# Sixteen-expert transformer layer on one core: four scattered tiles normalised one gate pair earlier, and one output product put off by a step

## The chip, the cores and the metric

The kernel runs on one NeuronCore of a Trainium2 chip, in one launch. The metric is the device time in microseconds (us). A profiled execution gives, beside that time, a span (first to last instruction) and a record of every instruction of every engine: PE (TensorE, with its weight loads as PEld), DVE (VectorE), ACT (ScalarE), POOL (GpSimd) and SP (SyncE, which here only issues DMAs).

## The reference, cut to what matters

Four blocks follow each other on x of 2048 rows (8 batches of 256) by 512 columns, each with a layer norm in front and a residual sum behind. Only the last two are near the change.

```python
x = x + _L0_xattn_ref(ctx_2048, ctx_2048, _layernorm(x, axis=-1), ...)
x = x + _L0_ffn_ref(_layernorm(x, axis=-1), ...)
x = x + _L1_xattn_ref(_layernorm(x, axis=-1), ctx_2048, ...)   # 16 heads, then out @ Wo + bo
x = x + _L1_ffn_ref(_layernorm(x, axis=-1), ...)
```
```python
def _L1_ffn_ref(x, wa, rg, rgb, rw1, rb1, rw2, rb2, sg, sgb, sw1, sb1, sw2, sb2):
    # each expert: (gelu(x @ g + gb) * (x @ w1 + b1)) @ w2 + b2, 512 -> 256 -> 512
    aff = jax.nn.sigmoid(jnp.einsum('bsd,de->bse', x, wa))
    topk_p, topk_i = jax.lax.top_k(aff, K)          # K = 2 of E = 16
    topk_p = topk_p / jnp.sum(topk_p, axis=-1, keepdims=True)
    combine = jnp.sum(jax.nn.one_hot(topk_i, E, dtype=x.dtype) * topk_p[..., None], axis=2)
    routed = jnp.einsum('bsed,bse->bsd', _experts_all(x, rg, rgb, rw1, rb1, rw2, rb2), combine)
    shared = jnp.sum(_experts_all(x, sg, sgb, sw1, sb1, sw2, sb2), axis=2)   # SH = 2 shared experts
    return x + shared + routed
```

## The kernel before, in words

The 2048 rows are 16 tiles of 128 (tile t is half t % 2 of batch t // 2) and stay in on-chip memory as `xs`. Every engine works its instructions off in a fixed order: inside an `in_order` block the order in the code is the order on PE, DVE, ACT and POOL. So an instruction that waits holds up all that is behind it on its engine.

**Attention (steps).** `steps` has 64 entries: batch b, half i, column pair cp, part p. The loop over n (lines 1363 to 1440 or so) runs a software pipeline: in pass n, POOL normalises the probabilities of step n-1 (`normalise`, L1275, fed by DVE's reciprocal `rden`, L1273), scores of new steps are made (`scores`, L1250), the probabilities of step n-2 are transposed on PE (`turn`, tile `pt`, L1286, copied out by DVE L1293 and ACT L1291), every second pass the value product (`values`, tile `o`, L1305, copied by ACT into `oT`, L1309) of step n-3 runs, and when step n-4 was the last of a half, `project_out` multiplies `oT` by Wo (tile `fo`, L1317, four times 128x512) and DVE adds `fo` to `xs` (L1320). A dictionary `put_off` names halves whose `project_out` waits for a later pass, counted from the start of the last batch; before the change it holds one, `(B - 2, 0): 1`. In the last eight passes and behind them (`at` = n - 56), the first eight tiles are also normalised for the next block by ACT (L1414), transposed on PE (tile `dxT`, L162) and copied by DVE (L1353). The tiles `o`, `fo` and `dxT` share two PSUM buffers ("mm"). After the loop, PSUM is handed to the next pool, whose first products (`lgT`, L1527) wait for DVE's last add.

**Shared experts and routing.** For the first eight tiles (tb 0 and 1) the two shared experts run: for each (tb, e, f) a pair of products `gate` (tile `gu`, L1546: four 128x512 matmuls each, which the trace shows as eight records), ACT's Gelu (L1558) and DVE's `gated` (L1559, tile `yT`). Between the pairs the generator `route` (pieces) is advanced with `next(pieces)`: six pieces work out the two experts of every row and the place `slot` of each row in a buffer `xd` in DRAM; then 16 pieces, one for each tile t, in each of which DVE normalises the tile (L1512, tile `dxs`, a ring of 8 buffers), POOL issues two indirect DMAs that scatter its rows to `xd` (L1675), and DVE brings the tile of `xs` itself to its normalised residual form (L1683). A last piece, called the tail here (L1689 to L1698: `over`, `past`, `expf`, `expert`), works out which expert each overflow block belongs to.

Then `down` (tile `po`, L1568) makes the eight down products, one for each tile of tb 0 and 1, eight records each, and DVE adds each to `xs` (L1572). `po` has four PSUM buffers: the fifth product must wait for the add of the first. After each of the first two down products up to two pieces are taken, as long as there are any.

**Routed experts.** SP loads the scattered rows (`r_xr`, L1710), reads `expert` into registers and loads weights; PE then runs 21 units (`turn`, `products`, `back`). At the end the second half of the shared experts runs while POOL gathers the routed rows.

What the change and the prediction touch: L1357 (`put_off`), L1847 (the counts of pieces), L1273, L1275, L1286, L1305, L1309, L1317, L1320, L1353 in the attention, and L1512, L1559, L1568, L1572, L1675, L1683, L1689 to L1698, L1884 (POOL's sum of the shared biases to every tile) behind it.

## Time and profile before

| | |
|---|---|
| time, median of 3 runs | 1144.72 us (1142.27 to 1147.37) |
| the profiled execution's own time | 1144.64 us |
| its span | 1142.8 us |
| PE busy | 1097.9 us, 96% of the span |
| DVE busy | 685.5 us, 60% |
| ACT busy | 519.4 us, 45% |
| POOL busy | 445.8 us, 39% |
| PE clock granted | 9 tenths or more in all 40 slices |
| HBM traffic | 107.66 MB read, 44.43 MB written |

The profiled execution's time is 1.8 us above its span, and within 0.1 us of the median of the runs. "Busy" is the time in which an engine has an instruction under way; "idle before" in a row is how long the engine had nothing before it, with what ended that idle time behind the arrow. In a timeline, rows of the same kind that follow each other are merged: "13.90 ... x32" is one stretch of 32 records. Source lines are those of the kernel before; in the changed kernel every line from 1355 on is one lower, since an empty line was taken out.

### The profile page before, as it was taken

What the parts mean: (1) busy time and instruction counts of PE and PEld (TensorE: products, weight loads), DVE (VectorE), ACT (ScalarE), POOL (GpSimd) and SP (SyncE); (2) the same over time, 40 slices, a digit from 0 to 9 for tenths busy, and PEclk for the clock granted to TensorE, in tenths of its full rate; (3) what the DMA queues carried; (4) which work ended last, traced back from release to release, by engine and by line L of the source; (5) the groups of instructions that cost most, each with busy time, mean ns of one, the idle gap of its engine ahead of it and who ended that gap; (6) DMA issues with size and microseconds to landing.
All of it is one profiled execution on the core that took longest, in us unless ns stands there. A gap on an engine that the chain in (4) does not pass through costs nothing.

```text
span 1142.8 us, 16506 instructions
## 1 busy us (share of the span) xinstructions
PE 1097.9 (96%) x5885; PEld 659.4 (58%) x5885; DVE 685.5 (60%) x1507; ACT 519.4 (45%) x1176; POOL 445.8 (39%) x501
## 2 busy tenths in 40 slices
PE   4999998899999999999999999899999999999997
PEld 3777776445545555555555555554466666675443
DVE  5998999899865565765656756647332222212452
ACT  4437645798984655756556557530011121111000
POOL 5787887245531333433333435413770000000650
PEclk9999999999999999999999999999999999999999
DMA  7424520799500100000000010053568999997571
GB/s 271 158 75 143 162 75 20 239 304 291 145 1 19 38 1 17 4 19 1 20 19 1 2 37 1 1 195 119 223 206 294 304 331 337 298 309 238 158 248 40
DMA packets 122780, 153.26 MB, mean 134 GB/s; under 512 B 7481, under 2 KB 81273, under 8 KB 122178
## 3 DMA queue, kind: packets, MB, share of 16 engines
q1 hardware_dynamic: 108608, 116.49, 32.2%
q10 hardware_dynamic: 8962, 18.85, 4.6%
q0 software_dynamic: 5120, 16.78, 4.3%
q8 instruction: 49, 0.80, 0.3%
q14 instruction: 41, 0.34, 0.1%
HBM read 107.66 MB, written 44.43 MB: 133 GB/s over the span
## 4 chain that ended last, share of the span: by engine, by line
PE 73%; DVE 19%; POOL 2%; issue 2%; ACT 2%; DMA 0%; ACTq 0%; POOLq 0%; DVEq 0%
PE r_h L1731 10%; PE gu L1546 10%; PE y L713 5%; PE v_mm L885 5%; PE r_po L1747 5%; PE q_mm L885 5%; PE po L1568 4%; PE f_op L493 4%; PE k_mm L885 3%; PE fo L1317 3%; PE pt L1286 3%; PE f_hp L409 3%; DVE mx L1258 2%; PE sc L1250 2%; PE o_h L1788 2%
## 5 line engine op out<-in xcount | busy, mean ns | idle before, releaser
L1275 POOL TENSOR_TENSOR pr<-pr,rden 128x1024 f32<-128x1024 f32 x64 | 121.1, 1893 | 218.9 <-DVE rden L1273 213.3
L713 PE MATMUL y<-kv,tp 128*128 128x288 f32 x640 | 161.7, 408 | 5.3 <-DVE wl L736 5.1
L713 PEld LDWEIGHTS y<-kv,tp 128*128 128x128 f32 x640 | 119.0, 190 | 42.5 <-PE y L713 10.1
L1266 ACT ACTIVATE pr<-sc,mx 128x256 f32<-128x256 f32 x256 | 118.3, 483 | 8.2 <-DVE mx L1258 6.9
L1889 POOL DMA_INDIRECT yg<-yd,slot x32 | 32.9, 1030 | 222.7 <-PE gu L1546 204.4
L1731 PE MATMUL r_h<-r_xT,r_gu 128*128 128x256 f32 x512 | 113.5, 380 | 0.0
L1731 PEld LDWEIGHTS r_h<-r_xT,r_gu 128*128 128x128 f32 x512 | 96.9, 190 | 20.6 <-issue 8.0
L1258 DVE TENSOR_REDUCE mx<-sc 128x4 f32<-128x1024 f32 x64 | 77.6, 1213 | 4.7 <-PE sc L1250 4.5
L1738 DVE SCALAR_TENSOR_TENSOR r_y<-r_h,eb,r_ge 128x256 f32<-128x256 f32 x32 | 15.5, 484 | 95.5 <-PE r_h L1731 95.5
L1286 PE MATMUL pt<-ident,pr 128*128 128x128 f32 x512 | 69.6, 279 | 2.2 <-POOL pr L1275 1.3
L1291 ACT COPY pts<-pt 128x512 f32<-128x512 f32 x64 | 37.8, 591 | 69.3 <-PE pt L1286 69.3
L1286 PEld LDWEIGHTS pt<-ident,pr 128*128 128x128 f32 x512 | 55.1, 140 | 19.1 <-issue 14.6
L1737 ACT ACTIVATE r_ge<-r_h,gb 128x256 f32<-128x256 f32 x32 | 15.1, 473 | 108.9 <-PE r_h L1731 108.9
L409 PE MATMUL f_hp<-w1q,f_xq 128*128 128x512 bf16 x256 | 60.5, 379 | 2.6 <-ACT f_h L422 1.5
L651 POOL TENSOR_TENSOR kv<-kx 128x2048 f32<-128x2048 f32 x16 | 57.6, 3601 | 13.1 <-ACT kx L637 13.1
L1317 PE MATMUL fo<-Wo_sb,oT 128*128 128x512 f32 x128 | 57.9, 595 | 1.1 <-ACT oT L1309 1.0
L885 PE MATMUL k_mm<-Wk_sb,cx 128*128 128x512 f32 x128 | 58.1, 598 | 0.6
L493 PE MATMUL f_op<-w2q,f_hq 128*128 128x512 bf16 x256 | 57.9, 379 | 0.0
L885 PE MATMUL v_mm<-Wv_sb,cx 128*128 128x512 f32 x128 | 57.7, 593 | 0.0
L1747 PE MATMUL r_po<-r_w,r_y 128*128 128x512 f32 x128 | 57.7, 593 | 0.0
L885 PE MATMUL q_mm<-Wq_sb,xT 128*128 128x512 f32 x128 | 57.6, 593 | 0.0
L1558 ACT ACTIVATE ge<-gu,gb 128x512 f32<-128x512 f32 x16 | 11.0, 687 | 100.6 <-PE gu L1546 71.9
(487 smaller groups left out, 2116.9 us busy)
## 6 DMA issues: line engine op xcount, KB each, us to landing
xd<-blank SPq DMA_DIRECT2D x1, 15360.0 KB
tp<-kpd SPq DMA_DIRECT2D x32, 256.0 KB
r_gu<-in_rg SPq DMA_DIRECT2D x16, 512.0 KB
r_gu<-in_rw SPq DMA_DIRECT2D x16, 512.0 KB
r_w<-in_rw SPq DMA_DIRECT2D x16, 512.0 KB
r_xr<-xd SPq DMA_DIRECT2D x16, 512.0 KB
yd<-r_yo ACTq DMA_DIRECT2D x32, 256.0 KB
yd<-blank SPq DMA_DIRECT2D x1, 6144.0 KB
```

Source lines behind the costliest of these rows:

```text
L409: nc.tensor.matmul(dst, lhsT=self.xq[:, i, c, :], rhs=w1q[:, c, cols], start=(c == 0), stop=False)
L493: nc.tensor.matmul(op, lhsT=self.hq[i][:, c, :], rhs=w2q[:, c, :], start=(c == 0), stop=(c == FC - 1))
L713: nc.tensor.matmul(y[:, ll, :, 0:PAIRS], lhsT=tp[:, dl : dl + P], rhs=view(kv, (m0 * G + hh) * PAIRS, [[G * PAIRS, B], [1, PAIRS]]), start ...
L885: nc.tensor.matmul(t, lhsT=lT[:, c, i * P : (i + 1) * P], rhs=w[:, c, :], start=(c == 0), stop=(c == DC - 1),)
L1258: nc.vector.tensor_reduce(self.mx, self.sc.rearrange("p r c k -> p (r c) k"), AX.X, ALU.max, negate=True)
L1266: nc.scalar.activation(self.pr[:, h // 2, h % 2, :], self.sc[:, h // 2, h % 2, :], AF.Exp, bias=self.mx[:, h : h + 1], accum_out=self.den[ ...
L1275: nc.gpsimd.tensor_tensor(flat, flat, rden.unsqueeze(2).to_broadcast([P, 4, S]), ALU.mult)
L1286: nc.tensor.transpose(pt[:, cc, k, :], self.pr[:, rr, cc, k * P : (k + 1) * P], ident)
L1317: nc.tensor.matmul(fo, lhsT=oT[:, c, :], rhs=wsb["Wo"][:, c, :], start=(c == 0), stop=(c == DC - 1))
L1546: nc.tensor.matmul(ps, lhsT=w[0][:, c, k, f * P : (f + 1) * P], rhs=xTs[tb][:, c, :], start=(c == 0), stop=(c == DC - 1),)
L1731: nc.tensor.matmul(ps, lhsT=self.w[0][:, c, k, f * P : (f + 1) * P], rhs=self.xT[:, c, 0:n], start=(c == 0), stop=(c == DC - 1),)
L1747: nc.tensor.matmul(po, lhsT=self.y[:, f, i * P : (i + 1) * P], rhs=self.w[1][:, f, :], start=(f == 0), stop=(f == EC - 1),)
```

## The change

Two numbers of the program's order are changed. The instructions of every engine are the same in number and kind; only their order on PE, DVE, ACT and POOL differs in two places, and SP's queue is the same.

```diff
-
-        put_off = {(B - 2, 0): 1}
+        put_off = {(B - 2, 0): 1, (B - 1, 0): 8}
...
     rest = [(tb, e, f) for tb in range(2) for e in range(SH) for f in range(EC)][2:]
-    for (tb, e, f), n in zip(rest, (0, 2, 3, 3, 3, 3)):
+    for (tb, e, f), n in zip(rest, (0, 2, 3, 3, 4, 4)):
         first_gate = gate(tb, e, f, shw[e], 0)
         for _ in range(n):
             next(pieces)
```

The first: `project_out` of half 0 of the last batch moves from pass n = 63 to n = 64. On PE this is the `fo` product of four 128x512 matmuls: before, it stood between the transposes `pt` of step 61 and the transposes `dxT` of tile 6; after, it stands behind the transposes of step 62 and the value product `o` of steps 60 and 61, ahead of `dxT` of tile 7 and `pt` of step 63. On DVE its add moves behind the copy of tile 6, the reciprocal of the last step and a copy of `pts`; on POOL nothing changes place.

The second: of the 16 scattering pieces, 3, 3, 3 and 3 stood in the four last gate pairs, two (tiles 12 and 13) behind them, and tiles 14 and 15 behind the first down product; the tail stood behind the second. After, 3, 3, 4 and 4 stand in the gate pairs, tiles 14 and 15 stand behind them ahead of all down products, and the tail stands between the adds of the first and the second down product. On DVE the order around the down products is then:

```
before: yT  t12 t13  po0  t14 t15  po1  tail  po2 po3 po4 ...
after:  (t10 t11 t12 t13) yT  t14 t15  po0  tail  po1 po2 po3 po4 ...
```

Here t12 stands for the pair L1512, L1683 of tile 12, and po0 for the add L1572 of the first down product.

## The prediction, made before the changed kernel was run

> **What bounds the kernel now.** I read the page's span and chain first, then the busy time by stage, then the timelines of PE, DVE and POOL around both edits.

> ```profile
> span 1142.8 us, 16506 instructions
> PE 73%; DVE 19%; POOL 2%; issue 2%; ACT 2%; DMA 0%; ACTq 0%; POOLq 0%; DVEq 0%
> 690.00:742.00 52.00, 47.77 (x472) 30.39 (x464) 35.13 (x68) 33.56 (x111) 24.51 (x14) 1.00 0.00 1
> 742.00:810.00 68.00, 67.41 (x243) 33.16 (x244) 39.34 (x95) 14.90 (x24) 22.18 (x40) 1.00 0.51 178
> 810.00:841.00 31.00, 27.99 (x65) 11.75 (x64) 13.85 (x21) 0.00 (x0) 23.12 (x22) 1.00 0.55 198
> 841.00:1050.00 209.00, 208.54 (x912) 143.89 (x910) 45.59 (x82) 38.99 (x79) 11.09 (x9) 1.00 0.90 297
> ```

> The stretches show length, then busy time of PE, PEld, DVE, ACT, POOL, the granted clock (1.00), DMA share and GB/s. From the end of the attention on, PE sets the time. The first edit lies at 726 to 742 us, the second at 800 to 841. Behind 841 PE waits 0.5 us in all until the end (its list of waits has one row there), so what PE gains or loses ahead of 841 goes through to the end unchanged. Of the 31 us with the down products PE is idle 3.0; that is all the second edit can win there, but for the refilling of PE after a wait.

> The end of the attention, PE, then POOL:

> ```profile
> 726.08 1.04 PE L1286 MATMUL pt<-ident,pr 128*128 128x128 f32 x8
> 728.12 3.70 PE L1317 MATMUL fo<-Wo_sb,oT 128*128 128x512 f32 x8 [1.00 <-ACT oT L1309]
> 731.65 0.60 PE L162 MATMUL dxT<-ident,dxn 128*128 128x128 f32 x4
> 732.09 1.04 PE L1286 MATMUL pt<-ident,pr 128*128 128x128 f32 x8
> 735.35 1.09 PE L1286 MATMUL pt<-ident,pr 128*128 128x128 f32 x8 [0.62 <-POOL pr L1275]
> 736.37 1.81 PE L1305 MATMUL o<-pts,v 128*32 128x128 f32 x32
> 738.11 3.70 PE L1317 MATMUL fo<-Wo_sb,oT 128*128 128x512 f32 x8
> ...
> 728.89 1.89 POOL L1275 TENSOR_TENSOR pr<-pr,rden 128x1024 f32<-128x1024 f32 x1 [4.11 <-DVE rden L1273]
> 733.40 1.90 POOL L1275 TENSOR_TENSOR pr<-pr,rden 128x1024 f32<-128x1024 f32 x1 [2.62 <-DVE rden L1273]
> ```

> The product that is moved (728.12) covers exactly the time in which POOL normalises the step whose transposes come next (728.89 to 730.78). The down products, PE, then DVE:

> ```profile
> 810.13 13.90 PE L1568 MATMUL po<-s_w,yT 128*128 128x512 f32 x32
> 824.87 3.70 PE L1568 MATMUL po<-s_w,yT 128*128 128x512 f32 x8 [0.85 <-DVE xs L1572]
> 829.14 3.70 PE L1568 MATMUL po<-s_w,yT 128*128 128x512 f32 x8 [0.57 <-DVE over L1689]
> 834.43 7.13 PE L1568 MATMUL po<-s_w,yT 128*128 128x512 f32 x16 [1.59 <-DVE xs L1572]
> ...
> 824.13 0.69 DVE L1572 TENSOR_TENSOR xs<-xs,po 128x512 f32<-128x512 f32 x1 [8.29 <-PE po L1568]
> 828.40 0.69 DVE L1572 TENSOR_TENSOR xs<-xs,po 128x512 f32<-128x512 f32 x1 [1.49 <-issue]
> 831.31 2.25 DVE L1697 TENSOR_SCALAR expf<-expf 128x56 f32<-128x56 f32 x1
> ```

> The four first products run through in 13.9 us, one each 3.43 us, so the first is done at about 813.7. DVE is free from 815.83 (end of tile 13's L1683), yet its add starts at 824.13, 0.1 us behind the end of the fourth product; the next waits another 1.49 us although its product was done at about 817.2. The last yT before them is late too: 812.97, for a gate product that ended at about 810.3. So most of PE's idle time here does not come from DVE's order, but from PE's completions reaching DVE late. The trace's record of PE's semaphore updates agrees: after 800 it has 812.88, 824.11, then 831.96, 832.05 and 832.14 together, with no product ending just before the first and the last three. I compared every wait of DVE and ACT for PE with the end of the matmul waited for; no other is over 0.4 us late.

> **First edit, the output product.** No instruction is added; I replay PE with the readiness times above. `pt` of step 61 ends at 727.12. Next is now `dxT` of tile 6: it takes the PSUM buffer that ACT's copy of `oT` releases at 728.07, so it runs 728.12 to 728.56. Next is `pt` of step 62, which needs POOL's product, done at 730.78: POOL started it at 728.89 because `rden` stood on DVE at 728.55 behind the batch's moments, and nothing of that is moved. So PE, which had 3.4 us of the moved product here, is idle 2.27 us (728.56 to 730.83). Then `pt` 1.0 and `o` 1.0 to 732.85, the moved `fo` 3.43 to 736.3 (its buffer: tile 6's copy, on DVE 731.6 to 732.3), `dxT` 0.43, `pt` of step 63 from 736.7 to 737.75. The wait of 0.62 for POOL is gone, as POOL starts that step at 732.5. The last `o` reads the `pts` that DVE copies; DVE now has the add of `fo` (736.55) and the copy of tile 7 (0.6 each) ahead of it, so the copy ends at 738.4 (736.73 before). 28 of the 32 products follow, 1.0 us: the last `fo` starts at 739.5, where it was 738.11. Sum: +1.4 us. POOL's sum of the bias (L1327, 1.26) moves behind the last normalisation and has until 742. Bounds: if both old waits went and no hole came, -1.6 (1.00 + 0.62); if the whole hole counts and the last `o` waits its 0.7 more, +3.0. I take +1.4, which the rows give in order.

> **Second edit, the tiles.** Per tile DVE has 0.54 + 0.55 us, in all 1.05 with the pitch; gate pairs take 6.87, and DVE is idle 2.9 us or more before each of the last yTs, so the fourth tile is covered. Each `dxs` needs a ring buffer whose scatter was issued eight tiles earlier: the latest, tile 15, needs tile 7's (its second scatter was issued by 807.66 and its completions stand at 809.4 at the latest) and comes at about 815. POOL's 32 scatters are 1.27 us apart and set its pace; DVE is ahead of them. POOL's only gap, 2.57 us before tile 14 (822.98 to 825.55), goes, so its scatters end 2.6 us earlier; SP's loads of `r_xr` (issued at 832.77, needed at 841.4) come as much earlier. Neither was on PE's path.

> What is on the path is when buffers of `po` come free. Here one thing is unknown: whether the late completions come again. Let the clock run from the first down product.
> - They come again at the same distances (first at 14.0 us, second at 18.3, third at 21.8): the fifth product starts at 14.74 as before. The tail follows the first add. It took 4.6 us before, of which L1697 took 2.25 for 56 elements a partition, beside two POOL additions (L1884, 831.01 to 833.50). Ahead of the scatters' end these POOL additions aren't there, so L1697 is put at 0.2, near its equal neighbours of 0.15 to 0.19 (L1689, L1698), and the tail at 2.5: 14.6 to 17.1. The second add comes at 18.3, the sixth product at 19.0 as before, the third add at 21.8, and the seventh product no longer waits (1.59 plus 0.1 to refill): -1.7.
> - They don't come: no buffer is ever late, the eight products take 8 x 3.43 = 27.5 instead of 31.3 (810.13 to 841.40): -3.8.
> I take -1.7, since the one execution shown has them; -3.8 and the slow rival's +4.7 are the bounds.

> Forecast: 1144.64 + 1.4 - 1.7 = 1144.3 us, no change.

> [...]

> **Rivals.** (a) The late completions are chance of this execution. Then the second edit gives -3.8 and the sum is 1144.64 + 1.4 - 3.8 = 1142.2. For it: no other wait of DVE or ACT for PE in the trace is late like this. Against: the execution's time equals the median of the others.

> (b) Slower. PE's completions reach DVE only where POOL's stream of scatters pauses: the first came at 824.11, in POOL's gap that tile 14 made, and the third to fifth after POOL's last scatter (830.98). The edit removes this gap: the stream then ends at 830.98 + 1.4 - 2.6 = 829.8, completions come about 1.0 later, at 830.8. PE has then been idle since 811.5 + 13.9 = 825.4; the fifth product starts at 831.5 (6.1 idle). Now the tail runs beside POOL's additions, 4.6 us, so the second add ends at 836.8 against the fifth product's end at 834.9: 1.9 more. With two refills of 0.25 that is 8.5 against 3.8: +4.7, and 1144.64 + 1.4 + 4.7 = 1150.7. It decides from the point where the first add starts later than 1 us behind the fourth product's end. Against: from 786 to 807 the scatters ran too and nothing was late.

> (c) The first edit makes no hole and both its waits go: -1.6, with (a) 1144.64 - 1.6 - 3.8 = 1139.2. Against: `rden` at 728.55 is fixed by DVE's order. That the change does not do what it says can't be: the built programs' orders show both moves.

> **How the numbers follow.** About 0.5% (5.7 us) is what a measurement of this kernel can tell from no change: 1139.0 to 1150.4. Forecast 0.48, (a) 0.26, (b) 0.16, (c) 0.10. Inside the 0.5% lie the forecast, (a), most of (c) and a little of (b). Faster by more: 0.07, the part of (c) and chance below 1139.0. Slower by more: 0.13 from (b). Range: from 1140.5, between (a) and (c), to 1149.5, short of (b).

> **What would show it.** The first edit: PE idle about 2.3 us ahead of the second-last `pt` of the attention, with POOL `pr` behind the arrow, and no wait at the last. The second: the first add of `po` ahead of the tail, L1697 short, no PE wait ahead of the seventh down product, and `r_xr` issued earlier. The forecast is wrong if a PE wait appears behind 841, or if the fifth down product waits longer than 0.85 us.

## The result, and the profile after

The changed kernel takes 1150.45 us (median of 6 runs, 1150.16 to 1151.5), the kernel before 1144.91 in the runs beside it (1142.27 to 1147.37). The ratio is 1.0050, with a 95% interval of 1.0034 to 1.0066: slower by 5.5 us. The forecast was 1144.3 us.

The profiled execution after has a span of 1148.7 us, 5.9 more than before. First the same stages as in the prediction (their bounds set anew, by hand, where the work lies now), then three short windows; columns are length, busy time of PE, PEld, DVE, ACT and POOL, granted clock, DMA share and GB/s.

```profile
span 1148.7 us, 16505 instructions
690.00:742.00 52.00, 46.81 (x467) 30.54 (x460) 34.71 (x67) 33.56 (x111) 24.55 (x14) 0.97 0.00 1
742.00:812.50 70.50, 69.72 (x249) 33.88 (x248) 41.65 (x99) 14.90 (x24) 22.04 (x40) 1.00 0.48 170
812.50:847.20 34.70, 29.88 (x66) 12.57 (x65) 11.03 (x17) 0.00 (x0) 22.91 (x22) 0.95 0.51 181
847.20:1056.00 208.80, 208.34 (x911) 143.78 (x909) 45.58 (x82) 38.99 (x79) 11.10 (x9) 1.00 0.90 297
722.87:726.29 3.42, 3.42 (x24) 2.35 (x20) 2.14 (x3) 0.85 (x3) 1.89 (x1) 0.50 0.00 0
832.10:835.51 3.41, 0.74 (x2) 0.30 (x2) 1.44 (x4) 0.00 (x0) 0.42 (x2) 1.00 0.42 145
835.51:838.93 3.42, 3.42 (x5) 1.35 (x4) 1.42 (x3) 0.00 (x0) 3.42 (x4) 0.50 0.84 263
```

From the first down product to `r_xTp` it is now 34.5 us (31.3 before), and twice PE ran at half its clock (0.50) for 3.4 us. The second time follows a window in which PE was busy for 0.74 of 3.41 us. Nothing of this kind lies in the span of the kernel before until its last microseconds.

The end of the attention, PE:

```profile
724.22 1.97 PE L1286 MATMUL pt<-ident,pr 128*128 128x128 f32 x8
727.68 1.04 PE L1286 MATMUL pt<-ident,pr 128*128 128x128 f32 x8
729.66 0.65 PE L162 MATMUL dxT<-ident,dxn 128*128 128x128 f32 x4 [0.94 <-ACT oT L1309]
731.80 1.33 PE L1286 MATMUL pt<-ident,pr 128*128 128x128 f32 x8 [1.50 <-POOL pr L1275]
734.07 3.70 PE L1317 MATMUL fo<-Wo_sb,oT 128*128 128x512 f32 x8
739.75 1.07 PE L1305 MATMUL o<-pts,v 128*32 128x128 f32 x28 [0.33 <-DVE pts L1293]
```

The hole that the prediction placed is there: PE waits for POOL's `pr` ahead of the second-last `pt`. The moved product stands at 734.07. The `pt` of 1.97 us at 724.22 ran at half clock; it lies ahead of the edit, and two kernels without this edit have such a stretch at the same place (e2 from 722.13, e11 from 721.91).

The down products, PE, then DVE:

```profile
812.77 13.90 PE L1567 MATMUL po<-s_w,yT 128*128 128x512 f32 x32
828.82 3.70 PE L1567 MATMUL po<-s_w,yT 128*128 128x512 f32 x8 [2.15 <-issue]
835.19 12.26 PE L1567 MATMUL po<-s_w,yT 128*128 128x512 f32 x24 [2.67 <-DVE xs L1571]
847.29 1.91 PE L162 MATMUL r_xTp<-ident,r_xr 128*128 128x128 f32 x16
...
817.64 0.75 DVE L1558 SCALAR_TENSOR_TENSOR yT<-gu,eb,ge 128x512 f32<-128x512 f32 x1 [6.39 <-PE po L1567]
828.08 0.69 DVE L1571 TENSOR_TENSOR xs<-xs,po 128x512 f32<-128x512 f32 x1 [7.51 <-PE po L1567]
830.98 1.30 DVE L1696 TENSOR_SCALAR expf<-expf 128x56 f32<-128x56 f32 x1
834.45 2.48 DVE L1571 TENSOR_TENSOR xs<-xs,po 128x512 f32<-128x512 f32 x4 [1.93 <-remote]
```

PE's work is unchanged, and its completions (the semaphore updates that tell DVE that a product is done) are late again, but the distances are longer: the first product is done at about 816.4 (812.77 + 3.6), its add starts at 828.08, 15.3 us behind the start of the first product (14.0 before); the second add comes at 21.7 us (18.3 before), and then four adds run at once. The fifth product waits 2.15 us (0.85 before).

What lies on POOL in that time, before and then after:

```profile
822.02 0.96 POOL L1675 DMA_INDIRECT xd<-dxs,slot  x1 [0.30 <-issue]
825.55 1.14 POOL L1675 DMA_INDIRECT xd<-dxs,slot  x1 [2.57 <-DVE dxs L1512]
...
828.70 0.96 POOL L1674 DMA_INDIRECT xd<-dxs,slot  x1 [0.30 <-issue]
829.97 0.96 POOL L1674 DMA_INDIRECT xd<-dxs,slot  x1 [0.30 <-issue]
830.95 1.28 POOL L1883 TENSOR_TENSOR xs<-xs,srow 128x512 f32<-128x512 f32 x1
```

Before, the first add (824.13) came in the pause that ends at 825.55. After, the scatters follow each other at 0.30 us up to 830.93; the first add came in the middle of them and the second 3.5 us behind their end.

So the 5.9 us of span are, in order: 1.0 for the half-clock window at 722.87 (it puts the `pt` behind the hole at 731.80, where e17 below, at full clock up to there, has it at 730.86), 1.6 for the hole in the attention (the first products behind it, `lgT`, start 2.64 later, less the 1.0), and 3.2 in the down products, of which 1.7 is the half-clock window at 835.51 (3.42 us at half speed). Behind 847 PE waits 0.5 us, as before.

### The profile page after: what moved, and what is told of

Its sections match the earlier page's. It is cut to its first block, busy times and chain, and to the rows that moved or that the text cites. A ratio compares the mean times of both kernels' runs of the same rounds, so it can differ in the third digit from the quotient of the medians.

```text
span 1148.7 us, 16505 instructions
## 1 busy us (share of the span) xinstructions
PE 1101.2 (96%) x5885; PEld 661.5 (58%) x5885; DVE 684.5 (60%) x1507; ACT 519.4 (45%) x1176; POOL 445.6 (39%) x501
## 4 chain that ended last, share of the span: by engine, by line
PE 74%; DVE 19%; POOL 2%; ACT 2%; issue 1%; DMA 1%; SPq 1%; another core or an unknown queue 0%; ACTq 0%; POOLq 0%; DVEq 0%
PE r_h L1730 10%; PE gu L1545 10%; PE y L713 5%; PE v_mm L885 5%; PE r_po L1746 5%; PE q_mm L885 5%; PE po L1567 5%; PE f_op L493 4%; PE k_mm L885 3%; PE fo L1317 3%; PE pt L1286 3%; PE f_hp L409 3%; DVE mx L1258 2%; PE sc L1250 2%; PE o_h L1787 2%; PE o L1305 2%
## 5 line engine op out<-in xcount | busy, mean ns | idle before, releaser
L1275 POOL TENSOR_TENSOR pr<-pr,rden 128x1024 f32<-128x1024 f32 x64 | 121.1, 1893 | 219.3 <-DVE rden L1273 211.6
L1286 PE MATMUL pt<-ident,pr 128*128 128x128 f32 x512 | 70.7, 281 | 3.0 <-POOL pr L1275 2.2
L1286 PEld LDWEIGHTS pt<-ident,pr 128*128 128x128 f32 x512 | 55.8, 142 | 20.5 <-issue 14.9
L1317 PE MATMUL fo<-Wo_sb,oT 128*128 128x512 f32 x128 | 57.9, 595 | 0.1
```

The lines of the kernel that those rows point to most:

```text
L1275: nc.gpsimd.tensor_tensor(flat, flat, rden.unsqueeze(2).to_broadcast([P, 4, S]), ALU.mult)
L1286: nc.tensor.transpose(pt[:, cc, k, :], self.pr[:, rr, cc, k * P : (k + 1) * P], ident)
L1317: nc.tensor.matmul(fo, lhsT=oT[:, c, :], rhs=wsb["Wo"][:, c, :], start=(c == 0), stop=(c == DC - 1))
```

## Experiments

Times are ratios to the kernel before, run beside each kernel on the same chip, with 95% intervals; "first add" is the start of the first `po` add, counted from the start of the first down product (3.6 is on time); "waits" is PE's idle time between the down products; "stage" runs from the first down product to `r_xTp`, both from the profile. A run without a ratio is one execution alone; e4, e7, e8, e9 and e16 leave scatters out or shorten them, so they do not compute the whole layer. e1 to e4 ran on one chip, e5 to e8 on a second, e9 to e12 on a third, e13 to e16 on a fourth, e17 and e18 on a fifth.

| run | ratio | span us | first add | waits | stage |
|---|---|---|---|---|---|
| before | | 1142.8 | 14.0 | 3.0 | 31.3 |
| after | 1.0050 (1.0034 to 1.0066) | 1148.7 | 15.3 | 4.8 | 34.5 |
| e1_putoff | 1.0023 (1.0008 to 1.0038) | 1147.6 | 13.3 | 3.3 | 33.2 |
| e2_counts | 1.0023 (1.0008 to 1.0039) | 1147.7 | 17.5 | 4.4 | 34.3 |
| e3_tail_late | 1.0037 (1.0023 to 1.0052) | 1152.1 | 11.8 | 5.0 | 35.7 |
| e4_scatter_8 | | 1142.2 | 3.6 | 0 | 27.5 |
| e5_eight_po | 0.9968 (0.9955 to 0.998) | 1140.9 | 16.3 | 0 | 28.4 |
| e6_counts_eight | 1.001 (0.9997 to 1.0022) | 1147.0 | 21.2 | 4.1 | 35.0 |
| e7_short_rows | | 1152.0 | 21.2 | 8.0 | 37.4 |
| e8_one_scatter | | 1141.7 | 10.7 | 0 | 27.5 |
| e9_last_eight | | 1142.2 | 3.6 | 0 | 27.5 |
| e10_code_shift | | 1161.2 | 3.6 | 0 | 27.5 |
| e11_counts_22 | 1.0001 (0.9991 to 1.001) | 1140.4 | 3.6 | 0 | 27.5 |
| e12_counts_22_eight | 0.9997 (0.9988 to 1.0007) | 1138.9 | 3.6 | 0 | 27.5 |
| e13_after_again | 1.0092 (1.0071 to 1.0114) | 1152.6 | 22.0 | 8.9 | 38.8 |
| e14_counts_22_again | 0.9973 (0.9958 to 0.9987) | 1139.1 | 7.2 | 0 | 27.5 |
| e15_counts_22_eight_again | 0.9971 (0.9956 to 0.9987) | 1139.2 | 6.5 | 0 | 27.5 |
| e16_last_eight_again | | 1141.5 | 3.6 | 0 | 27.5 |
| e17_putoff_22 | 0.9983 (0.997 to 0.9996) | 1142.5 | 10.3 | 0 | 27.7 |
| e18_counts_22_third | 0.9949 (0.9933 to 0.9965) | 1138.9 | 6.3 | 0 | 27.5 |

### Each edit alone, and the tail's place

```diff
# e1_putoff
-        put_off = {(B - 2, 0): 1}
+        put_off = {(B - 2, 0): 1, (B - 1, 0): 8}
# e2_counts
-    for (tb, e, f), n in zip(rest, (0, 2, 3, 3, 3, 3)):
+    for (tb, e, f), n in zip(rest, (0, 2, 3, 3, 4, 4)):
# e3_tail_late: both, and ahead of the tail
+        for _ in range(2):
+            yield
         nc.vector.tensor_copy(over, end[:, E : E + 1])
```

> Only the first edit: the output product of half 0 of the last batch is put off from step 63 to 64; the counts stay 3, 3. Theory A (each edit costs by itself; of the 5.9 us between the two profiled spans the first gives 1.6, the down products 3.3, and a half-clock stretch near 723 us the last 1.0): 1.0 to 2.0 us over the kernel before in the same job, with PE idle about 2 us ahead of the second-last pt and the sixteen tiles' scatters as before, the first add of po at about 14.0 us from the first down product. Rival B (the first edit shifts the routing against the down products and so causes the longer waits there too): 4 to 6 us over before, with the fifth down product waiting 2 us or more.

> Only the second edit: counts 3, 3 become 4, 4, the output product stays where it was. Theory A: 1.5 to 4 us over before, PE idle 2 us or more ahead of the fifth down product, again 2 us or more ahead of the sixth with DVE's add of po behind the arrow and the tail (over, past, expf, expert) ahead of that add; the attention as before. Rival B (the down products wait only when both edits meet): within 0.7 us of before or faster.

> The changed kernel, with two empty pieces ahead of the tail, so that the tail (over, past, expf, expert) stands behind the add of the second down product, where it stood before the change. If the tail's place is what delays the sixth product: 1.5 to 3 us below the changed kernel (1147.5 to 1149), with the second add right behind the first and no second wait. If the second completion of PE reaches DVE late by itself (as the third to fifth, which came together at 834.5 in the changed kernel's trace, 3.6 us behind the last scatter's end): within 0.7 us of the changed kernel, and the second add still stands at 21 us or more behind the start of the first down product, now with DVE idle before it.

Each edit alone costs 0.23%, 2.6 us, and the sum, 0.46%, agrees with the 0.50% of both within the intervals. For e1 that is more than theory A's 1.0 to 2.0; what the rest is, the pair e17 and e18 shows. (In e1's profile the down products are 1.9 us longer too; in that pair PE waits nowhere between them.) In e2 the first add comes at 17.5 us and the fifth product waits 4.4; the expected second wait is not there, since the fifth product ran at half clock (827.95 to 834.77) and so ended behind the second add (833.78). The late tail (e3) changes nothing that can be told (0.37%, against 0.50% for the changed kernel on another chip): the second add still stands 21.6 us behind the start, now with DVE idle for 9.2 us before it. The tail's place is not the cause.

### Is it POOL's stream of scatters?

```diff
# e4_scatter_8, on the changed kernel
-            for k in range(2):
+            for k in range(2 if t < 8 else 0):
# e8_one_scatter: range(2 if t < 8 else 1); e9_last_eight: range(0 if t < 8 else 2)
# e7_short_rows
-                    out=xd, out_offset=offset(ap=slot[:, k, t : t + 1], axis=0),
-                    in_=xn, in_offset=None,
+                    out=xd if t < 8 else xs32, out_offset=offset(ap=slot[:, k, t : t + 1], axis=0),
+                    in_=xn if t < 8 else xn[:, 0:32], in_offset=None,
```

> The changed kernel without the sixteen scatters of tiles 8 to 15 (their rows are then not in the scattered table; the normalising on DVE and everything else stays). Theory S (PE's completions reach DVE late while POOL's stream of scatters runs): with no scatter after about 800 us the last yT and all adds of po start within 0.4 us of the end of their products, the first add about 3.6 to 4.5 us from the start of the first down product, no wait of PE between the down products, and some 5 to 7 us less than the changed kernel (1143 to 1146). Rival D (late completions belong to PE and DVE at this place, whatever POOL does): the last yT is still 3 us late, the first add still stands at 14 us or more from the first down product.

> The changed kernel, whose scatters of tiles 8 to 15 move 32 of the 512 columns of each row, into a table of their own (so the rows of these tiles are not in the scattered table): as many scatters and descriptors on POOL, a sixteenth of the bytes. If the bytes that move hold PE's completions back: on time as without these scatters, the eight products in 27.6 us. If it is POOL's issue or the number of descriptors: the first add still 13 to 17 us behind the start of the first down product, PE waiting 2 us or more.

> The changed kernel with one scatter instead of two for tiles 8 to 15 (the second rows of these tiles are not in the table). If a stream without pauses is what holds completions back: the stream from 810 us on is half as long (eight scatters, about 10 us, over by 820 to 822), so completions are late up to then and on time from then: the first add 8 to 11 us behind the start of the first down product, before the fourth product has ended, and no wait of PE. If each completion waits for a fixed count of scatters or a fixed time: the first add still at 13 us or more.

Without the later sixteen scatters every completion is on time and PE runs the eight products in one stretch (e4, PE):

```profile
813.38 27.63 PE L1568 MATMUL po<-s_w,yT 128*128 128x512 f32 x64
```

With half of them (e8) the stream ends at 821.8, and the adds come at 823.52 and then together; those of products that end later are on time. The bytes are not the cause: with a sixteenth of them (e7) it is worse, the first add comes 3.2 us behind the last scatter's end (831.25). (`xs32` is a table of 32 columns.) Theory S (POOL's stream holds the completions back) stands, and theory D (it belongs to this place on PE and DVE) falls.

### Eight buffers: take away what makes PE wait

```diff
# e5_eight_po, on the kernel before; e6_counts_eight the same with counts 4, 4
-        po = pd.tile([P, D], F32, tag="po", name=f"po{t}")
+        po = pd.tile([P, D], F32, tag="gh" if tb == 1 else "po", name=f"po{t}")
```

> The kernel before, with the down products of tiles 4 to 7 in the four PSUM buffers of the gate products (tag gh), which nothing uses there, in place of a second turn of the four po buffers; orders of all engines as before. Theory S (the scatters hold back PE's completions, and PE loses time only because it needs a po buffer back): the adds still come 10 us late, but PE runs the eight products through in 27.6 us without a wait, and with no stretch of low PE activity there no half-clock window follows near 830 us: 3 to 6 us below before (1140 to 1142.5). Rival T (PE's wait only moves: r_xTp and the next gates need the gh buffers, whose adds are late): a new wait of 2 us or more ahead of r_xTp or of r_h, and within 1.5 us of before.

> The same eight buffers together with the second edit (counts 4, 4), without the first. Theory S: as with 3, 3 within 1 us, since what the second edit costs is only the longer wait for po buffers: 1140 to 1143. If the second edit costs something beside the buffers: 2 us or more above the run with 3, 3.

With counts 3, 3 the completions are as late as ever (first add 16.3 us), but PE has no buffer to wait for, and the kernel is 0.32% faster; 1.0 us of wait for `r_xr` is left ahead of `r_xTp`. With counts 4, 4 the expectation missed by 5 us: 1147.9 instead of 1140 to 1143. PE has buffers and still stops. Its rows in e6:

```profile
810.79 15.61 PE L1568 MATMUL po<-s_w,yT 128*128 128x512 f32 x36
827.05 0.59 PE L1568 MATMUL po<-s_w,yT 128*128 128x512 f32 x1 [0.65 <-issue]
829.14 0.59 PE L1568 MATMUL po<-s_w,yT 128*128 128x512 f32 x1 [1.50 <-issue]
830.54 0.92 PE L1568 MATMUL po<-s_w,yT 128*128 128x512 f32 x1 [0.81 <-issue]
```

After 36 records PE goes on one record at a time, waiting for nothing that the profile names, until the completions come through at 831.9. What the second edit costs is thus not only a buffer: it takes the pause out of POOL's stream. In e5 POOL paused for 4.90 us from 823.5, and six held completions came through together (PE's semaphore updates at 826.94 to 827.32); in e6 there was no pause, and they came at 831.93 and later, 3.2 us behind the last scatter.

### A pause in the right place: the opposite of the second edit

```diff
# e11_counts_22 (again: e14, e18); with eight buffers: e12, e15
-    for (tb, e, f), n in zip(rest, (0, 2, 3, 3, 3, 3)):
+    for (tb, e, f), n in zip(rest, (0, 2, 3, 3, 2, 2)):
# e10_code_shift, on the changed kernel
+    dm = pd.tile([P, TB], F32, tag="po", name="dm")
+    for _ in range(44):
+        nc.tensor.matmul(dm[:, 0:1], lhsT=ident, rhs=ident[:, 0:1], start=True, stop=True)
     pieces = route()
```

> The changed kernel with the scatters of tiles 8 to 15 alone (those of tiles 0 to 7 are left out, so these rows are not in the table): sixteen scatters, from about 802 to 822 us. If the number of scatters before counts (late only from the seventeenth on): the last yT, all adds of po on time, no PE wait. If the place counts, that is what PE does at this point: the last yT and the first add late as in the changed kernel, up to some 2 to 3.5 us behind the last scatter (first add 10 to 13 us from the start of the first down product).

> The changed kernel with 44 tiny products on PE (128x1, into a buffer nobody reads) ahead of the routing, about 745 us. They move the point at which PE's next block of instructions is fetched (16 KB packet on PE's instruction queue, 814.6 in the changed kernel, 2 us behind the start of the down products) some 19 us forward against PE's work, into the gate products of 792 to 800, where scatters run too. Theory F (completions are held back when a fetch of PE's code meets the scatters): late completions start there, gate products wait for gelu and yT, and DVE's normalising with them: the gates take several us longer than the 27 us they took. Theory C (it belongs to the later scatters or to the down products, whatever is fetched): the gates run as before and the last yT and first add of po are late as before.

> The opposite of the second edit, without the first: counts 2, 2 instead of 3, 3, so that tiles 12 and 13 wait for the first add of po and POOL's scatters pause some 5 us earlier (after tile 11, about 818). If a pause of POOL's stream lets the completions through 0.3 to 3.5 us later: the first add at 8 to 12 us from the start of the first down product instead of 14, the second at once behind it, no wait of PE ahead of the fifth and sixth products; the later adds are held again until the last scatter is through, and the seventh product waits 1 to 4 us. In time 2 us below to 1 us above before. If the pause has nothing to do with it: first add at 13 us or later again, and as everything behind it comes later, 3 us or more above before.

> Counts 2, 2 with the eight buffers for the down products. With the pause inside the stream, PE should run the eight products in 27.6 us without a wait; what remains is whether r_xr (loaded behind the last scatter) is in time for r_xTp. Within 1 us of the run with 3, 3 and eight buffers (1142 to 1144). If the later end of the scatters decides: a wait ahead of r_xTp of 2 us or more and 1145 or more.

In all four of these runs every completion was on time, also with a stream without pauses (e10, e11, e12), so they tell nothing of their questions (the span of e10 holds its tiny products and the half-clock stretch that they brought). They ran on a chip on which the kernel before took 1142.1 us (at most 1143.1), where it took 1145.5, 1145.9, 1145.2 and 1147.1 on the four others. So I ran the changed kernel again beside them on another chip.

> The changed kernel again, beside the next three on one chip. In the four runs of the job before this one no completion was late, and the kernel before took 1142.1 there (at most 1143.1) against 1145.5 and 1145.9 (up to 1149.9) on the two chips of the jobs before it. If lateness goes with the chip (theory X): on a chip with late completions (before above 1144.5) the changed kernel stands 4 to 7 us above before and its first add 13 us or more from the start of the first down product; on a chip without (before below 1143) its adds are on time, the eight products take 27.6 us and it stands only the first edit's 0.5 to 2.5 us above before. If the lateness of the earlier runs came from their programs and not from the chip: 4 to 7 us above before with a before of about 1142.

> Counts 2, 2 without the first edit, once more. On a chip with late completions: if a pause of POOL's stream lets them through, first add at 8 to 12 us, no wait ahead of the fifth and sixth products, a wait of 1 to 4 us ahead of the seventh, and 2 us below to 1 us above before; if not, first add at 13 us or later and 3 us or more above before. On a chip without: as before within 1 us.

> Counts 2, 2 with eight buffers for the down products, once more. On a chip with late completions: 3 us or more below before (no wait of PE between the down products, as with 3, 3 and eight buffers), and a wait ahead of r_xTp below 2 us. On a chip without: within 1.5 us of before, as PE has nothing to wait for there in either.

> The changed kernel with the scatters of tiles 8 to 15 alone, once more. On a chip with late completions: if the number of scatters before counts, everything on time; if the place counts, the last yT and the first add late, the add 10 to 13 us from the start of the first down product. On a chip without: on time, and nothing is learnt of this.

Here the completions were late again. The changed kernel lost 0.92%, 10 us; its last `yT` waited 13.07 us, and all four completions came through together (834.54 to 834.82), 4.0 us behind the last scatter's end (830.50). PE then ran at half clock for three windows, 829.48 to 839.72 (e13, DVE and PE):

```profile
824.09 0.75 DVE L1558 SCALAR_TENSOR_TENSOR yT<-gu,eb,ge 128x512 f32<-128x512 f32 x1 [13.07 <-PE po L1567]
834.56 0.69 DVE L1571 TENSOR_TENSOR xs<-xs,po 128x512 f32<-128x512 f32 x1 [7.63 <-remote]
...
812.53 13.90 PE L1567 MATMUL po<-s_w,yT 128*128 128x512 f32 x32
835.31 5.02 PE L1567 MATMUL po<-s_w,yT 128*128 128x512 f32 x6 [8.88 <-DVE over L1688]
```

With counts 2, 2 on the same chip nothing stops PE, and the kernel is 0.27% faster than before (e14), the same with eight buffers (e15). The order of events is plainest in e18 (POOL, DVE, PE):

```profile
811.41 0.96 POOL L1675 DMA_INDIRECT xd<-dxs,slot  x1 [0.30 <-issue]
814.34 1.14 POOL L1675 DMA_INDIRECT xd<-dxs,slot  x1 [1.98 <-DVE yT L1559]
...
812.86 0.75 DVE L1559 SCALAR_TENSOR_TENSOR yT<-gu,eb,ge 128x512 f32<-128x512 f32 x1 [6.60 <-remote]
816.35 0.69 DVE L1572 TENSOR_TENSOR xs<-xs,po 128x512 f32<-128x512 f32 x1 [0.65 <-remote]
831.97 1.88 DVE L1572 TENSOR_TENSOR xs<-xs,po 128x512 f32<-128x512 f32 x3 [5.13 <-PE po L1568]
...
810.01 27.63 PE L1568 MATMUL po<-s_w,yT 128*128 128x512 f32 x64
```

`yT` is late, the next tile's `dxs` stands behind it in DVE's order, so POOL has nothing to scatter after 812.37. Within half a microsecond of that pause the completion arrives (812.86), `dxs` follows, and POOL goes on after 1.98 us. Three adds get through in time; the later ones come at 831.97, 2.1 us behind the last scatter and still ahead of the eighth product (from about 834.0), the last one that needs a buffer back. With counts 4, 4 fourteen tiles stand ahead of the last `yT` in DVE's order, in place of ten; POOL has work through the whole lateness, and nothing pauses.

That a pause lets the completions through is the reading that fits all of this, but it is not shown by itself: POOL pauses because DVE waits, so pause and wait come together in every run here. And a pause is not needed for every completion: in ten profiles (before, after, e1, e2, e3, e5 to e8, e13) the one that the last `yT` waits for came in the middle of the scatters, 1 to 11 us late, and in after, e2 and e3 the one of the first add too.

e16 shows where it begins: with sixteen scatters alone (802.81 to 823.95) every add is on time, the first 3.6 us behind the start of the first product. In e13 the first late one is a product done at about 809.2, some 20 us and sixteen scatters into the stream. That a fetch of PE's instructions is what meets the scatters does not fit: in e16 the fetch (815.07) lay in the middle of the stream and nothing was late, and in e13 it came (814.54) behind the first late product.

### The first edit by itself

```diff
# e17_putoff_22: the first edit with counts 2, 2
-        put_off = {(B - 2, 0): 1}
+        put_off = {(B - 2, 0): 1, (B - 1, 0): 8}
```

> The first edit (output product put off) with counts 2, 2, where PE does not wait between the down products: what the first edit costs by itself. Prediction's own sum: 1.4 us above the same kernel without it (run beside it here), with PE idle about 2 us ahead of the second-last pt; half-clock stretches at 722 to 737 us may add or take 1 to 2 us. If the 2.65 us of the first edit alone came from the down products and not from the attention: within 0.7 us.

> Counts 2, 2 without the first edit, as the pair of the run above on the same chip: 1140.5 to 1142 on any chip, 3 to 4 us below before where completions are late (before above 1144.5), as before within 1 us where they are not.

Medians 1144.24 and 1140.96: the first edit costs 3.3 us, with no PE wait between the down products in either. The windows, first e17, then e18, show both parts of it:

```profile
728.40:731.80 3.40, 1.34 (x12) 1.01 (x10) 2.12 (x9) 3.18 (x12) 1.89 (x1) 1.00 0.02 5
731.80:735.22 3.42, 3.42 (x36) 2.23 (x35) 1.06 (x3) 0.96 (x2) 1.89 (x1) 0.50 0.00 0
```

```profile
728.40:731.80 3.40, 3.40 (x11) 1.54 (x10) 1.82 (x9) 3.06 (x11) 1.89 (x1) 1.00 0.00 0
731.80:735.22 3.42, 2.81 (x48) 2.20 (x45) 2.46 (x5) 0.96 (x2) 1.94 (x2) 1.00 0.00 0
```

In the first window PE is idle for 2.06 us with the edit and not at all without it; the second then runs at half clock (0.50), where it has the full one without the edit. In it `o` takes 1.94 instead of 1.08 and `fo` 4.41 instead of 3.70, 1.6 us. The products behind (`lgT`) start at 745.62 and 742.47; of these 3.15, 0.15 was there ahead of the edit and 1.6 is the clock, so the hole alone is 1.4. (The other 0.2 us between the two kernels is a later `r_xTp`, 27.7 against 27.5.)

The other profiles agree. Eleven have the first edit: in three of them (after, e4, e7) the half clock came early, at 722, and not again at the hole; the other eight all have it at the hole, starting between 729.86 and 732.10. Of the nine without the edit none has it there.

In the profiles every half-clock stretch ahead of the last few microseconds lasts 3.41, 6.83, 10.24 or 17.07 us: one, two, three or five times 3.41. The two after begin 112.64 us apart (722.87 and 835.51), 33 times 3.41. So I laid a grid of 3.41 us windows through the stretches of each profile; it lies differently in each (a window begins at 731.80 in e17, at 829.48 in e13) and gives PE's busy share ahead of every fall. Half clock came behind windows in which PE was busy for up to 0.67 of the time (719.46 to 722.87 after). Between the first 20 us and the last few microseconds, full-clock windows with PE busy for 0.40 or less were always followed by half clock (0.22 ahead of 835.51 after, 0.39 ahead of 731.80 in e17), those between 0.41 and 0.67 sometimes, fuller ones never; a window already at half clock was in four runs followed by another although PE was busy for 0.89 to 0.96 of it (e2, e4, e7, e11; the 44 products of 128x1 in e10 aside, which brought 17.07 us of half clock). So the same hole went unpunished in the changed kernel's profile: the work ahead of it had come late by the half-clock window at 722.87, only 1.50 us of the hole were left, and the share of its window (729.70 to 733.11) was 0.56. That is luck of the grid.

## Why the prediction was wrong

- **First edit, +1.4.** Right as a replay of PE: the hole, its place, the vanished wait of 0.62 and a last `o` waiting for `pts` (0.33) are all there, and the pair gives 1.4. What the sum left out, a term put at nothing, is that a hole of 2 us can cost a half-clock window behind it, 1.6 more; together 3.0 of the 3.3 us between e17 and e18. In the changed kernel's own profile the two parts are 1.6 and 1.0, the 1.0 from the window at 722.87.
- **Second edit, -1.7: the step that failed is "They come again at the same distances (first at 14.0 us, second at 18.3, third at 21.8)".** The distances are not a property of the products. They go with POOL's stream of scatters: without its second half nothing is late (e4), and what is held comes through together once it ends. The edit takes out the pause in which the first add came, and the adds stand at 15.3 and 21.7 us in the profile after, the first at 17.5 in e2 and 22.0 in e13. Alone the edit costs 2.6 us (e2), where -1.7 was forecast; its opposite gains 3.1 and 5.9 (0.27% and 0.51%: e14, e18).
- **Rival (b)** had this mechanism and 1150.7 us, against 1150.45 measured. That the number came so near is luck: it had +1.4 and +4.7 where the edits alone cost 2.6 each. It put the first add at 830.8 (828.08) and PE's wait for it at 6.1 us (2.15), and knew nothing of the half-clock window that makes 1.7 of the 3.2 us. I gave it 0.16 because "from 786 to 807 the scatters ran too and nothing was late". That is true and proves nothing: sixteen scatters alone do no harm (e4, e16).
- **Rival (a)**, late completions as chance, holds in one sense: on one of the five chips of the experiments, four kernels had none. There the kernel before took 1142.1, and counts 2, 2 gained nothing (1.0001). The argument against it, that the profiled time equals the median, was weak: three runs of the kernel before spread from 1142.27 to 1147.37, and on the chip of e13 to e16 it took from 1140.29 to 1148.97 in 23 runs. So the lateness may change from one execution to the next as well; no trace shows the others.
- **The tail.** L1697 was put at 0.2; it took 1.30 after, beside POOL's additions (they began at 830.95), since the first add came too late for it. In both traces it ends 0.05 to 0.06 us behind POOL's addition (833.56 and 833.50 before, 832.28 and 832.23 after). e3 shows that its place does not matter.
- **The scatters' lengths.** The sum has no term for them. Before, they took 0.96 to 1.46 us each, and the rows tie the long ones to no single work of DVE: the 1.46 (829.52) stands beside the tail, and one beside the normalising (797.36) took 0.96.
- **What held:** PE's wait behind 847 (0.5), no wait ahead of the seventh product, and the scatters' end 2.7 us earlier against the down products (18.2 us behind the first one's start, 20.9 before; forecast 2.6).

Beyond both kernels: the counts 2, 2 without the first edit (e11, e14, e18) take 1141.0 to 1141.5 us on three chips: 0.51% and 0.27% below before on two, and the same as before on the chip without late completions.

Open: what in the chip holds PE's completions back while POOL issues scatters, and why one chip shows none of it. The bytes moved (e7) and the fetch of PE's code (e16) are excluded; the path itself was not tried, nor a pause of POOL that does not come from DVE's wait.

## What to carry to other kernels

When a wait in a trace ends long after the work it waits for, do not carry its duration into a forecast: find what was running all that time on another engine and ask whether the edit lengthens it. On the kernel's side, an order in which the waiting engine also feeds the other one's stream (counts 2, 2) gained 0.27% and 0.51% on the two chips with such waits and cost nothing on the one without; working ahead (counts 4, 4) kept the waits up. And PE's idle time is not worth its own length alone: a hole of 2 us cost 1.4 itself and 1.6 through the clock.
